# A softmax maximum turned on VectorE instead of TensorE, and value sums added on the way to DRAM

## The chip, the cores and the metric

The kernel runs on one core of one Trainium2 chip. The metric is the device time of one execution in microseconds (us). The engines are named as in the profile: PE (TensorE, the matrix engine), DVE (VectorE), ACT (ScalarE), POOL (GpSimd) and SP (the sync engine, which here only issues DMAs). "PEld" is PE's loading of weights, which overlaps its matmuls. DMAs are issued by SP, ACT and POOL, each with a queue of its own; a queue's engine issues in program order, so a DMA that must wait holds up those behind it.

## The reference

One block of a diffusion transformer on x of shape (2, 2048, 576), in fp32, with 16 heads of D = 36:

```python
ada = silu(c) @ W_ada + b_ada
shift_msa, scale_msa, gate_msa, shift_mlp, scale_mlp, gate_mlp = split(ada, 6)
h = layernorm(x) * (1 + scale_msa) + shift_msa
q, k, v = split(h @ W_qkv + b_qkv, 3)              # 16 heads of 36
attn = softmax((q * 36**-0.5) @ k.T)               # 2048 keys
x = x + gate_msa * ((attn @ v) @ W_proj + b_proj)
h = layernorm(x) * (1 + scale_mlp) + shift_mlp
x = x + gate_mlp * (gelu_tanh(h @ W_fc1 + b_fc1) @ W_fc2 + b_fc2)
```

The softmax takes off a maximum before the exponential. The kernel works with scores that lie keys by queries, so that maximum (one for each query) runs across partitions.

## The kernel before

**Front.** Up to about 270 us the kernel makes the ada vectors, the queries, keys and values of the first batch element (generators `queries_keys_values`, `stages`) and gated copies of two weights. Beside the stages runs a generator `later()`: each `next(rest, None)` in the stages' loop lets it go on to its next `yield`. It loads two sixths of W_ada (`wa`, L202 to L204), yields, clears a PSUM tile (`cleared(2)`), yields, and then makes the rows of ada from it (`rows_of`, matmul L425, tile `pa`), which the gates need.

**Main loop.** The rest is one loop over steps G. A unit is one head of one block of 512 queries (QB); there are NU = 128 units, and each takes NG = 4 steps g = 0 to 3. A step treats 512 of the 2048 keys, two tiles of 128 from each half of them. In one step PE makes the scores of unit su, two units ahead (L648, tile `s`, PSUM), then some matmuls of other work, then the weighted sum of values of the present unit u (L719, tile `av`). The other work is taken from a list: projections of the second batch element (`pq`, `pv`), and for each block whose heads are done the output projection (`po`), the MLP (`pf` L1172 and `py` L1220) and its gathering. `fill()` takes work while a credit lasts, in every even step and in odd ones if the credit is high.

The other engines, for one unit and group of keys:

- ACT copies the scores to SBUF (L661, tile `e`, 128x1024, twice).
- DVE takes the running maximum of them into `acc` (`maxima`, L666). After the fourth group it takes the larger of its two halves (128x512), which leaves for each query 128 candidates, one in each partition.
- In the next step (g = 0 for the present unit, variable `chain`) PE turns these 128x512 by four transposes into PSUM (`turn`, L684, tile `mt`, which takes a buffer of the scores' pool). DVE reduces them to 128x4 (`across`, L694, tile `mx`). SP writes this to DRAM (L695, `m_d`) and reads it back as a broadcast over all partitions (L698, tile `m`, 128x512, two buffers).
- DVE subtracts `m` from the scores (`less`, L703), two steps ahead of PE's use; ACT takes the exponential in place (L707), one step ahead; PE uses it.

`av` has two banks, one for each row half of the array, and in each bank the two halves of the keys lie in partitions 0 to 36 and 64 to 100. So four partial sums are to be added. After the last group `take` has ACT copy one bank to SBUF (L731, tile `up`, one buffer) and DVE add the other (L732). `store`, put off to the end of the next step, has SP write the lower part to DRAM (L738 `o_d`, L739 `sum_d`) and POOL add the upper part to it by accumulating DMAs (L740, L741). Row 0 of each part is the sum of exponentials (`sum_d`), rows 1 to 36 the values.

When the last head of a block is stored, `gather` reads `sum_d` and `o_d` back (L1047 to L1057), loads x with the bias (L820, L824), takes the reciprocal (L1062), writes it (L1063, `rec_d`) and reads it back as broadcasts (L1075, tile `r`) for a multiplication on DVE (L1084). These DMAs are POOL's.

SP's order in a unit: keys and queries of a unit ahead (`kT`, `qT`, L169 and L170), `mx` out (L695), `m` in (L698), then the present store (L738, L739).

Of the kernel before, what the change touches and what calls it, by code (L numbers as in the profile page):

```python
# [10 lines left out]
F32 = mybir.dt.float32  # L11
AF = mybir.ActivationFunctionType
ALU = mybir.AluOpType
AX = mybir.AxisListType
# [3 lines left out]
P = 128  # L18
# [4 lines left out]
def dit_block_kernel(  # L23
# [16 lines left out]
    nc = tc.nc  # L40
# [9 lines left out]
    QB = 512  # L50
    NQB = L // QB
    TB = QB // P
    HA = D + 1
# [3 lines left out]
    NG = HALF // (2 * P)  # L57

    def seq(ins):

        return tc.keep_in_program_order(ins)
# [21 lines left out]
    m_d = [scratch.tile([P, TB], F32, name=f"m_d{u}") for u in range(NB * H)]  # L83

    ident = const.tile([P, P], F32, name="ident")
# [88 lines left out]
    with ExitStack() as front:  # L174
# [200 lines left out]
        def load_in(n):  # L375
# [22 lines left out]
            out=of_b,  # L398
            in_=ident.rearrange("p (k q) -> p q k", k=NC)[:, 0:B, :],
            op=ALU.add,  # L400
            axis=AX.X,
# [3 lines left out]
        def cleared(part):  # L405
            pa = wide(f"pa_{part}")
            seq(nc.vector.memset(pa[:, :, :C2], 0.0))
            return pa
# [108 lines left out]
        def later():  # L517
# [4 lines left out]
            for b in range(B):  # L522
                for i, src in enumerate((b_fc2, b_proj)):
                    at = ds(64 * b + 32 * i, 1)
                    seq(nc.gpsimd.dma_start(out=lines[at, :], in_=src.unsqueeze(0)))
            yield
            yield
            yield
            pas[2] = cleared(2)
            yield  # L530
            g1 = []
# [8 lines left out]
            for b in range(B):  # L540
                seq(nc.vector.tensor_scalar_mul(half[b], g2[b], 0.5))
                for i, (to, g) in enumerate(((gb_d, g2), (gp_d, g1))):
                    at = ds(64 * b + 32 * i, 1)
# [55 lines left out]
    with ExitStack() as main_part:  # L599
# [12 lines left out]
        class Unit:  # L612
# [50 lines left out]
            def maxima(self, g):  # L663

                one, two = (self.es[g][:, j].rearrange("p i n -> p (i n)") for j in range(2))
                top = lambda out, x, y: seq(nc.vector.tensor_max(out, x, y))  # L666
                if g == 0:
                    self.acc = np_.tile([P, 2 * QB], F32, tag="acc", name=f"acc_{self.u}", bufs=1)
                    top(self.acc, one, two)
                    return  # L670
                a = self.acc
                top(a, a, one)
                top(a, a, two)
                if g == NG - 1:
                    self.am = a[:, :QB]
                    top(self.am, a[:, :QB], a[:, QB:])

            def turn(self):

                room = ps_s.tile([P, 2, 512], F32, tag="s", name=f"mt_{self.u}")  # L680
                self.pt = room[:, 0, :].rearrange("p (i n) -> p i n", i=TB)
                for i in range(TB):
                    seq(
                        nc.tensor.transpose(  # L684
                            self.pt[:, i, :],
                            self.am.rearrange("p (n i) -> p i n", i=TB)[:, i, :],
                            ident,
                        )
                    )

            def across(self):

                mx = np_.tile([P, TB], F32, tag="mx", name=f"mx_{self.u}")
                seq(nc.vector.tensor_reduce(out=mx, in_=self.pt, op=ALU.max, axis=AX.X))  # L694
                seq(nc.sync.dma_start(out=m_d[self.u], in_=mx))  # L695
                self.m = np_.tile([P, QB], F32, tag="m", name=f"m_{self.u}")
                flat = m_d[self.u].rearrange("p i -> (p i)")
                seq(nc.sync.dma_start(out=self.m, in_=flat.partition_broadcast(P)))  # L698

            def less(self, g):  # L700
# [26 lines left out]

            def take(self):

                self.up = np_.tile([P, QB], F32, tag="up", name=f"up_{self.u}", bufs=1)  # L730
                seq(nc.scalar.copy(self.up, self.av[:, 0, :]))  # L731
                seq(nc.vector.tensor_add(self.up, self.up, self.av[:, 1, :]))  # L732

            def store(self):

                o, sums = o_d[self.blk][ts(self.h, D), :], sum_d[self.blk][ds(self.h, 1), :]
                lo, hi = self.up[:HA, :], self.up[64 : 64 + HA, :]
                seq(nc.sync.dma_start(out=o, in_=lo[1:HA, :]))  # L738
                seq(nc.sync.dma_start(out=sums, in_=lo[0:1, :]))  # L739
                seq(nc.gpsimd.dma_start(out=o, in_=hi[1:HA, :], accum_op=ALU.add))  # L740
                seq(nc.gpsimd.dma_start(out=sums, in_=hi[0:1, :], accum_op=ALU.add))  # L741

        NT3 = 3
        state = {"wpr": None, "turn": 0, "slot": None, "norm": None}
# [567 lines left out]
        def subtract(G):  # L1312
            if 0 <= G < NU * NG:
                units[G // NG].less(G % NG)
# [17 lines left out]
        for G in range(-AHEAD, NU * NG + 1):  # L1332
# [5 lines left out]
                units[su + 1].load_keys()  # L1338
            if g == 1 and -1 <= u and u + 1 < NU:
                units[u + 1].load_values()  # L1340
            cu, cg = divmod(G - 1 + AHEAD, NG)
            chain = cg == NG - 1 and 0 <= cu < NU
            count(RATE)
            forced = g % 2 == 0 or G < 0 or credit > RATE
            tiles = units[su].scores(sg) if su < NU else None
# [8 lines left out]
            if 0 <= G + 1 < NU * NG:  # L1354
                lu, lg = divmod(G + 1, NG)
                units[lu].exps(lg)
            if chain:
                subtract(G + 2)
                units[cu].turn()
            for last in lasts:  # L1360
                last()
            lasts.clear()
            if 0 <= G < NU * NG:
                units[u].weigh(g)
            if chain:
                units[cu].across()
                if tiles:
                    units[su].maxima(sg)
            elif g == NG - 2:
                if tiles:  # L1370
                    units[su].maxima(sg)
                subtract(G + 2)
            else:
                subtract(G + 2)
                if tiles:
                    units[su].maxima(sg)
            flush()
# [75 lines left out]
```

## Time and profile before

| what | value |
|---|---|
| runs (three) | 3707.89, 3703.1, 3703.63 us, median 3703.63 |
| profiled execution | 3707.24 us, span 3705.5 us |
| granted TensorE clock | 0.999 |
| instructions | 59239 |
| DMA | 382.13 MB, mean 103 GB/s |
| ACT: copy of scores L661 | 1024 of 1025 ns |
| DVE: subtraction L703 | 512 of 2276 ns |
| DVE: maximum L666, 128x1024 | 896 of about 1222 ns |

The profile is of one execution; its own time is 3.6 us above the median of the runs. A row of a group gives the line, the engine, the operation, output and input tiles, their shapes and the count, then the busy time in us and the mean ns of one, then the engine's idle time just before these instructions and what ended it. In a timeline a row starts with its start and its length in us, counted from the start of the span; "x24" joins 24 instructions.

### The profile page before, as it was taken

The page shows a single profiled execution, that of the slowest core. Times are in us where ns is not written, and L with a number is a line of the kernel's source. Part 1 is how long each engine was busy: PE and PEld are TensorE (multiplying, and loading weights), DVE is VectorE, ACT ScalarE, POOL GpSimd, SP SyncE. Part 2 cuts the span into 40 slices and gives each one's busy share as a digit, 9 for nine tenths or more (in the row PEclk, how much of TensorE's full clock was granted, in tenths as well). Part 3 has the DMA queues.
Part 4 walks back from the last instruction along what each step waited for, and adds up shares of the span by engine and source line. Part 5 has one row for each costly group of instructions (what it writes and reads, how often), then busy time and mean ns, then how long its engine had stood idle before and what let it go on. Part 6 is the DMA issues. An engine that isn't in the chain of part 4 may idle for free.

```text
span 3705.5 us, 59239 instructions
## 1 busy us (share of the span) xinstructions
PE 3682.3 (99%) x23926; PEld 1722.0 (46%) x23926; DVE 2948.0 (80%) x3000; ACT 2327.3 (63%) x2166; POOL 706.2 (19%) x1044
## 2 busy tenths in 40 slices
PE   8999999999999999999999999999999999999999
PEld 4554344444444534454444444453444444444565
DVE  4627889889888888888889888988889888988422
ACT  0006767668776677667667777767667767676321
POOL 0101121222122111311131212211130213111411
PEclk9999999999999999999999999999999999999999
DMA  7733333544244343524353424424352435342522
GB/s 245 267 110 105 100 99 96 119 116 111 67 109 112 76 90 80 126 66 99 79 133 70 113 65 114 108 60 105 76 126 67 99 82 120 80 97 61 136 71 70
DMA packets 426946, 382.13 MB, mean 103 GB/s; under 512 B 315591, under 2 KB 316633, under 8 KB 426673
## 3 DMA queue, kind: packets, MB, share of 16 engines
q0 software_dynamic: 77248, 205.28, 20.5%
q1 hardware_dynamic: 82928, 129.54, 12.5%
q10 hardware_dynamic: 266496, 43.53, 7.2%
q8 instruction: 189, 3.10, 0.4%
q14 instruction: 85, 0.69, 0.1%
HBM read 306.98 MB, written 71.21 MB: 102 GB/s over the span
## 4 chain that ended last, share of the span: by engine, by line
PE 94%; DMA 3%; DVE 1%; ACT 1%; issue 1%; POOL 0%; SPq 0%; DVEq 0%; ACTq 0%; POOLq 0%
PE av L719 23%; PE s L648 22%; PE py L1220 15%; PE pf L1172 14%; PE po L799 4%; PE pq_q L975 3%; PE pq L278 3%; PE pf L104 2%; PE pv L328 2%; PE pv_q L799 2%; PE mt L684 2%; DMA x_b<-gp_d 1%; PE po L104 1%; DMA wa<-in_L_cond_W_ada_dram 1%; DVE acc L666 0%
## 5 line engine op out<-in xcount | busy, mean ns | idle before, releaser
L661 ACT COPY e<-s 128x1024 f32<-128x1024 f32 x1024 | 990.2, 1025 | 813.3 <-PE s L648 802.7
L703 DVE TENSOR_TENSOR e<-e,m 128x2048 f32<-128x2048 f32 x512 | 1162.8, 2276 | 9.8 <-DMA m<-m_d 9.8
L666 DVE TENSOR_TENSOR acc<-acc,e 128x1024 f32<-128x1024 f32 x768 | 939.5, 1223 | 171.9 <-ACT e L661 127.7
L707 ACT ACTIVATE e<-e 128x2048 f32<-128x2048 f32 x512 | 991.2, 1936 | 0.9 <-DVE e L703 0.8
L719 PE MATMUL av<-e,v 64*64 64x512 f32 x8192 | 981.3, 594 | 0.1
L648 PE MATMUL s<-qT,kT 36*64 36x512 f32 x8192 | 973.4, 589 | 2.1 <-DVE mx L694 1.1
L1220 PE MATMUL py<-w,gT 128*128 128x288 f32 x2304 | 580.2, 410 | 0.0
L648 PEld LDWEIGHTS s<-qT,kT 36*64 36x64 f32 x8192 | 313.1, 133 | 571.3 <-issue 522.8
L719 PEld LDWEIGHTS av<-e,v 64*64 64x64 f32 x8192 | 296.0, 133 | 510.0 <-issue 460.3
L1172 PE MATMUL pf<-h_b,w_b 128*128 128x512 f32 x1152 | 530.7, 605 | 0.0
L1220 PEld LDWEIGHTS py<-w,gT 128*128 128x128 f32 x2304 | 432.4, 190 | 175.4 <-issue 37.2
L740 POOL DMA_DIRECT2D o_d<-up x128 | 109.3, 854 | 1969.8 <-DMA o_d<-up 1439.2
L1172 PEld LDWEIGHTS pf<-h_b,w_b 128*128 128x128 f32 x1152 | 208.2, 190 | 318.0 <-issue 303.7
L694 DVE TENSOR_REDUCE mx<-mt 128x4 f32<-128x512 f32 x128 | 88.2, 689 | 169.9 <-PE mt L684 169.9
L1183 ACT ACTIVATE gT<-pf,bias 128x512 f32<-128x512 f32 x144 | 99.1, 688 | 193.0 <-PE pf L104 132.7
L1192 DVE SCALAR_TENSOR_TENSOR th<-th,gT 128x1024 f32<-128x1024 f32 x72 | 88.1, 1223 | 90.0 <-ACT th L1190 89.8
L666 DVE TENSOR_TENSOR acc<-e 128x1024 f32<-128x1024 f32 x128 | 155.6, 1216 | 4.4 <-ACT e L661 4.4
L1232 DVE TENSOR_TENSOR x_b<-py,x_b 128x288 f32<-128x288 f32 x192 | 81.5, 452 | 84.2 <-PE py L1220 84.2
L741 POOL DMA_DIRECT2D sum_d<-up x128 | 144.0, 1125 | 1.0 <-issue 1.0
L799 PE MATMUL po<-wpr_p,oT 128*128 128x288 f32 x512 | 132.6, 413 | 0.0
L278 PE MATMUL pq<-hT,w_in 128*128 128x512 f32 (+1 forms) x320 | 129.2, 555 | 0.0
L766 POOL DMA_DIRECT2D w_b<-in_L_cond_W_fc_dram x72 | 73.8, 1025 | 266.9 <-PE pf L1172 242.9
(156 smaller groups left out, 2453.2 us busy)
## 6 DMA issues: line engine op xcount, KB each, us to landing
w<-w_d POOLq DMA_DIRECT2D x72, 576.0 KB, 6.1
v<-v_d ACTq DMA_DIRECT2D x128, 296.0 KB
kT<-qk_d SPq DMA_DIRECT2D x256, 144.0 KB
w_b<-in_L_cond_W_fc_dram POOLq DMA_DIRECT2D x72, 512.0 KB, 4.6
m<-m_d SPq DMA_DIRECT2D x128, 256.0 KB
qT<-qk_d SPq DMA_DIRECT2D x256, 72.0 KB
w_d<-wg POOLq DMA_DIRECT2D x12, 864.0 KB, 8.4
qk_d<-ev SPq DMA_DIRECT2D x36, 256.0 KB
```

The costliest lines, as they stand in the source:

```text
L104: nc.tensor.matmul(outs[r][ts(c, 64), :], lhsT=lefts[r][:, ts(c, 64)], rhs=rights[r], start=starts[r], stop=not starts[r],)
L278: nc.tensor.matmul(pq[:, r, :n], lhsT=w_in[:, kc, cols], rhs=hT[:, kc, at], start=(kc == 0 and not (two and r)), stop=(kc == KC - 2 and tw ...
L648: nc.tensor.matmul(s[ts(c, 64), i, :], lhsT=self.kT[at, ds((2 * g + j) * P + 64 * c, 64)], rhs=self.qT[at, :], start=True, stop=True,)
L661: seq(nc.scalar.copy(self.es[g][:, j], s))
L666: top = lambda out, x, y: seq(nc.vector.tensor_max(out, x, y))
L703: seq(nc.vector.tensor_sub(e, e, m))
L707: seq(nc.scalar.activation(e, e, AF.Exp))
L719: nc.tensor.matmul(self.av[ts(i, 64), r, :], lhsT=self.v[ts(r, 64), ds((c + i * (HALF // P)) * HA, 64)], rhs=e[ts(r, 64), j, i, :], start= ...
L741: seq(nc.gpsimd.dma_start(out=sums, in_=hi[0:1, :], accum_op=ALU.add))
L799: nc.tensor.matmul(outs[n][:, :C2], lhsT=src[:, kc, ts(i, P)], rhs=w_[:, kc, ts(n, C2)], start=(kc == 0), stop=False,)
L1172: nc.tensor.matmul(pfs[j], lhsT=wc[:, kc, ts(j, P)], rhs=h2[:, kc, :], start=(kc == 0 and j == 0), stop=(kc == KC - 2 and j == 1),)
L1220: nc.tensor.matmul(py[n][:, :C2], lhsT=gTs[f - f % 2][:, f % 2, ts(i, P)], rhs=w2s[f - f % 2][:, f % 2, ts(n, C2)], start=(j == 0), stop=( ...
```

## The change

The maximum is turned on DVE. After the last group `maxima` calls `across` at once: DVE transposes the 128x512 in squares of 32x32, reduces each to 128x16, copies the four partition groups of 32 side by side, reduces again to 32x16 and lets SP write this to DRAM. Nothing of it is left on PE. The broadcast read is a step of its own, `load_maxima`, in step g = 1, after the subtraction there, and `m` has one buffer. `take` is one copy of both banks on ACT, and `store` writes one part by SP and adds three by POOL. In the front `later()` has two yields more before `cleared(2)`.

```diff
@@ def later():
             yield
+            yield
+            yield
             pas[2] = cleared(2)
@@ class Unit, maxima
                 if g == NG - 1:
-                    self.am = a[:, :QB]
-                    top(self.am, a[:, :QB], a[:, QB:])
-
-            def turn(self):
-                room = ps_s.tile([P, 2, 512], F32, tag="s", name=f"mt_{self.u}")
-                self.pt = room[:, 0, :].rearrange("p (i n) -> p i n", i=TB)
-                for i in range(TB):
-                    seq(
-                        nc.tensor.transpose(
-                            self.pt[:, i, :],
-                            self.am.rearrange("p (n i) -> p i n", i=TB)[:, i, :],
-                            ident,
-                        )
-                    )
-
-            def across(self):
-                mx = np_.tile([P, TB], F32, tag="mx", name=f"mx_{self.u}")
-                seq(nc.vector.tensor_reduce(out=mx, in_=self.pt, op=ALU.max, axis=AX.X))
-                seq(nc.sync.dma_start(out=m_d[self.u], in_=mx))
-                self.m = np_.tile([P, QB], F32, tag="m", name=f"m_{self.u}")
+                    top(a[:, :QB], a[:, :QB], a[:, QB:])
+                    self.across(a)
+
+            def across(self, a):
+                v = a[:, QB:].rearrange("p (i n) -> p i n", n=32)
+                seq(nc.vector.transpose(v, a[:, :QB].rearrange("p (n i) -> p i n", n=32)))
+                n16 = QB // 32
+                mq = a[:, :n16]
+                seq(nc.vector.tensor_reduce(out=mq, in_=v, op=ALU.max, axis=AX.X))
+                m4 = a[:32, n16 : 5 * n16].rearrange("p (r i) -> p r i", r=4)
+                for r in range(4):
+                    seq(nc.vector.tensor_copy(m4[:, r], mq[ts(r, 32), :]))
+                mx = np_.tile([32, n16], F32, tag="mx", name=f"mx_{self.u}")
+                by_query = m4.rearrange("p r i -> p i r")
+                seq(nc.vector.tensor_reduce(out=mx, in_=by_query, op=ALU.max, axis=AX.X))
                 flat = m_d[self.u].rearrange("p i -> (p i)")
+                seq(nc.sync.dma_start(out=flat.rearrange("(n i) -> n i", n=32), in_=mx))
+
+            def load_maxima(self):
+                flat = m_d[self.u].rearrange("p i -> (p i)")
+                self.m = np_.tile([P, QB], F32, tag="m", name=f"m_{self.u}", bufs=1)
                 seq(nc.sync.dma_start(out=self.m, in_=flat.partition_broadcast(P)))
@@ take, store
-                self.up = np_.tile([P, QB], F32, tag="up", name=f"up_{self.u}", bufs=1)
-                seq(nc.scalar.copy(self.up, self.av[:, 0, :]))
-                seq(nc.vector.tensor_add(self.up, self.up, self.av[:, 1, :]))
+                self.up = np_.tile([P, 2, QB], F32, tag="up", name=f"up_{self.u}", bufs=1)
+                seq(nc.scalar.copy(self.up, self.av))
...
-                lo, hi = self.up[:HA, :], self.up[64 : 64 + HA, :]
-                seq(nc.sync.dma_start(out=o, in_=lo[1:HA, :]))
-                seq(nc.sync.dma_start(out=sums, in_=lo[0:1, :]))
-                seq(nc.gpsimd.dma_start(out=o, in_=hi[1:HA, :], accum_op=ALU.add))
-                seq(nc.gpsimd.dma_start(out=sums, in_=hi[0:1, :], accum_op=ALU.add))
+                for r in range(2):
+                    for at in (0, 64):
+                        part = self.up[at : at + HA, r, :]
+                        for to, rows_ in ((o, part[1:HA, :]), (sums, part[0:1, :])):
+                            if r == 0 and at == 0:
+                                seq(nc.sync.dma_start(out=to, in_=rows_))
+                            else:
+                                seq(nc.gpsimd.dma_start(out=to, in_=rows_, accum_op=ALU.add))
@@ main loop
-            cu, cg = divmod(G - 1 + AHEAD, NG)
-            chain = cg == NG - 1 and 0 <= cu < NU
...
-            if chain:
-                subtract(G + 2)
-                units[cu].turn()
             for last in lasts:
                 last()
             lasts.clear()
             if 0 <= G < NU * NG:
                 units[u].weigh(g)
-            if chain:
-                units[cu].across()
-                if tiles:
-                    units[su].maxima(sg)
-            elif g == NG - 2:
+            if g == NG - 2:
                 if tiles:
                     units[su].maxima(sg)
                 subtract(G + 2)
             else:
                 subtract(G + 2)
+                if g == 1 and -1 <= u and u + 1 < NU:
+                    units[u + 1].load_maxima()
                 if tiles:
                     units[su].maxima(sg)
```

## The prediction

> **What bounds the kernel now.** I read the page's busy shares first.
>
> ```profile
> span 3705.5 us, 59239 instructions
> ## 1 busy us (share of the span) xinstructions
> PE 3682.3 (99%) x23926; PEld 1722.0 (46%) x23926; DVE 2948.0 (80%) x3000; ACT 2327.3 (63%) x2166; POOL 706.2 (19%) x1044
> ```
>
> TensorE (PE) has 23 us without work in the whole span, so a microsecond of PE work taken away is a microsecond of time, unless another engine then falls behind. Next come the groups by line and shape, for what the diff touches.
>
> ```profile
> L684 PE MATMUL mt<-ident,acc 128*128 128x128 f32 x512 | 81.6, 282 | 4.9 <-DVE acc L666 3.0 <-ACT e L661 1.9
> ...
> L694 DVE TENSOR_REDUCE mx<-mt 128x4 f32<-128x512 f32 x128 | 88.2, 689 | 169.9 <-PE mt L684 169.9
> ...
> L732 DVE TENSOR_TENSOR up<-up,av 128x512 f32<-128x512 f32 x128 | 87.5, 683 | 17.6 <-ACT up L731 17.5
> ```
>
> The last two numbers of a row are the engine's idle time before it and who ended it: VectorE (DVE) loses 169.9 us waiting for PE's transposes. Busy PE time overlaps at its modelled ends, so I price the transposes by start times in a timeline of PE, one pair of steps without and one with them.
>
> ```profile
> 1522.42 6.09 PE L1220 MATMUL py<-w,gT 128*128 128x288 f32 x24
> 1528.44 1.95 PE L719 MATMUL av<-e,v 64*64 64x512 f32 x16
> ...
> 1535.47 6.09 PE L1220 MATMUL py<-w,gT 128*128 128x288 f32 x24
> 1541.39 0.63 PE L684 MATMUL mt<-ident,acc 128*128 128x128 f32 x4
> 1541.96 1.52 PE L719 MATMUL av<-e,v 64*64 64x512 f32 x12
> ```
>
> From py to av it is 6.02 us without the four transposes and 6.49 with them: 0.47 us of the path per unit. Last, two windows behind places where PE does wait (length; busy time of PE, PE's weight loads, DVE, ACT, POOL; then the granted clock, DMA share, GB/s), and the SP queue around one unit's end.
>
> ```profile
> 2737.00:2741.00 4.00, 3.88 (x22) 1.59 (x26) 4.00 (x5) 0.00 (x0) 1.26 (x3) 0.63 0.39 109
> ```
> ```profile
> 40.80:44.80 4.00, 3.99 (x21) 1.14 (x22) 0.29 (x1) 0.00 (x0) 0.00 (x0) 0.59 1.04 361
> ```
> ```profile
> 1516.21 0.34 SPq L695 DMA_DIRECT2D m_d<-mx  x1
> 1522.06 0.34 SPq L698 DMA_DIRECT2D m<-m_d  x1
> 1522.46 0.90 SPq L738 DMA_DIRECT2D o_d<-up  x1
> ```
>
> The first window follows a wait of 1.93 us for DVE before transposes at 2737.12, the second a wait of 3.11 us for ada weights (wa) before L425 at 40.81; in both the clock is granted at 0.6 for 4 us afterwards. The SP rows show that a unit's store, ready when L732 ended at 1509.68, leaves at 1522.46 only, behind the load of the maximum, which waits for mx to land.
>
> **The change, part by part.**
>
> *Transposes off PE.* 128 units x 0.47 us = 60.2 us of pure path. With them go PE's waits before them, 4.9 us, and a wait of scores for mx, 1.1 us (list of waits: "PE s L648 <- DVE mx L694"). After the 1.93 us wait 4.00 us ran at 0.63, so 1.5 us more were lost there. Sum 67.7 us.
>
> *Two yields in the front.* In the new order the third pair of query-key matmuls (16 + 8, some 8 us) stands ahead of the ada rows that waited; its weights were sent before wa on the same queue. The rows come 8 us later, when wa (landed by 40.8) is there. Gain 3.1 us and, at 0.59 for 4.00 us, 1.6 us: 4.7. If another load is late there, it is 0.
>
> [...]
>
> *DVE's new chain.* Removed per unit: 0.69 (L694) + 0.68 (L732). Added: a 32x32 transpose of 128x512, a reduction of 128x512, four copies of 32x16, a reduction of 32x64. The reduction has its row, 0.69. No transpose is in the trace: the shortest row of that size is a one-source 128x576 at 454 ns, the nearest above that could stand for a slow pass is 128x2048 at 2.28 us; I take 0.69, that of both 128x512 rows with SBUF input and of the reduction. Copies lie between a memset of 128x16 (72 ns) and a copy of 128x22 (173 ns): 0.16 each. The last reduction lies between 128x8 (159 ns) and 128x512 (689 ns): 0.22. Sum 2.24 us (1.6 to 4.4), net +0.87 per unit (+0.2 to +3.0), +111 us on DVE: 3059, still 84% of a span of 3635. Against that DVE no longer waits for mt and up (169.9 + 17.5 us, 1.46 per unit). The tightest common stretch is a unit like 1314.0 to 1336.6: PE full, DVE 21.28 busy and 1.0 waiting for mt. Afterwards DVE needs 22.15 in 22.13: even. Three such units stand in a row and then units of 26 us with DVE at 22 follow. The pair of subtractions at 1325.23 is taken by ScalarE (ACT) 2.7 and 4.6 us after each is done, at 1330.23 and 1334.32, and the first of these is done 4.5 us before PE uses it (1336.62): that covers the 0.02, and nearly also 2.2 us a unit at the upper end. Cost 0; with the transpose at its upper end up to 2 us in each of 8 blocks, 16.
>
> [...]
>
> *One buffer of m.* The load is issued after the last subtraction of the unit before (step 1) instead of at once, and SP waits there; behind it SP has only the next mx, two steps later. First use is the subtraction of step 2. Between them DVE does four maxima: 1520.26 to 1525.46, 5.2 us. A load landed in 3.00 us in the chain (897.44), and 1522.06 to 1525.46 held one without idle time, so it is hidden by about 2 us. The slowest like it, the 288 KB broadcast x_b<-gp_d, takes 8.8: then DVE idles 3.6 us, which its slack of about 4 us a unit takes up. Cost 0 (0 to 10 us in all).
>
> *The take.* ACT copies 128x1024 (1025 ns, as L661) for 128x512 (589): +56 us on ACT, 63 to 66%. It then frees av by itself, some 0.3 us earlier than copy and add did; the next av is 5 us off. Cost 0.
>
> *Stores.* Per unit four more POOL DMAs, 2 x 0.85 + 2 x 1.13 = 4.0 us, so POOL goes from 706 to 1213 us, 33%. Each add to o_d waits for the one before it: issue to landing 2.7 us (2.1 to 6.6). From the take's end: SP's store 2.7, two adds of 0.5 + 2.7, the third's issue 0.5 and behind it the last sum, 0.6 + 2.6: 12.8 us. But the store is no longer behind the load of m and leaves at about 1509.7 instead of 1522.46, so the chain ends near 1522.5, where now it ends at 1526.74 + 0.6 + 2.6 = 1530. The buffer up, single, is wanted by the next take at 1534.99: 12 us of cover. Behind the adds on POOL stand weight loads of the next steps, no later than now. In a block's second unit the adds stand behind r loads that wait for rec_d (1522.73), so the chain ends near 1533 and the cover is 2 us, with the other r loads 3 us later. 8 blocks at 0 to 3 us: I take 3 us in all. The gather of each block starts some 1.5 to 8 us earlier, which takes the r loads out of the wait that led to 2737.
>
> **Sum.** 67.7 + 4.7 - 3 = 69.4 us off. The profiled execution took 3707.24 us around a span of 3705.5; its runs have a median of 3703.63, 3.6 lower. 3707.24 - 69.4 = 3637.8, on the median 3634.2.
>
> **Rivals.** *Part of it comes back* (12%): PE is free earlier than DVE and ACT can feed it. For it: units at 97% DVE (unit span 2509.6 to 2532.3, 21.9 of 22.65). Against it: 188 us of DVE waits fall away. Price: 16 us there with the long transpose, 24 in the blocks' second units and no 4.7 in the front leave 69.4 + 3 - 44.7 = 27.7 us, 3676, so 3660 to 3690. *The stores decide, slower* (9%): the place is the single buffer up, ACT's take waiting for the fourth landing. The chain holds 3.1 us of copy, issues and wake-ups and four landings L in a row. A unit takes 24.6 us (tile m's uses run from 312.2 to 3457.2, over 128), 24.1 without transposes; with 3 us of slack behind the take the chain exceeds it at L = 6.0, and the gain of 0.54 us a unit is eaten at L = 6.15. At the largest landing of the trace, 6.6, it would be 2.4 us x 128 = 307 us, 3940. Against it: the median is 2.7; for it: three times as many adds share the queue. *The diff's PE saving was cover for something else* (2%): PE waits the 0.47 us elsewhere, 3703. *More* (5%): the transposes are worth their busy 81.6 us, 3613 or less.
>
> **How the numbers follow.** The forecast, 3615 to 3660, has 72%. The range 3615 to 3672 adds about half of the partial case and leaves some 20% outside. Faster by over 0.2% (7 us, about what a measurement of this kernel can tell from no change) is 72 + 12 + 5 = 89%, within it 2%, slower 9%.
>
> **What would show it.** Right: no group mt on PE, PE still at 99% of a span near 3633 and its busy time near 3610; DVE near 3060 us with an idle time before L666 that names ACT, the transpose near 0.7 us; the SP store about 1 us after the take; the row at 40.81 without its wait. Wrong: ACT's copy of up waiting for o_d or sum_d for over 100 us in all, DVE's subtraction waiting for m for over 100 us, PE's idle time above 50 us, or a transpose of over 4 us.

## The result and the profile after: 59 us slower, not 69 us faster

The changed kernel takes 3765.15 us (median of 5 runs, 3762.57 to 3772.67) beside 3705.88 us for the kernel before (5 runs, 3703.1 to 3711.14). The ratio is 1.0161, 95% interval 1.0146 to 1.0176. The prediction was 3634 us, with a range of 3615 to 3672. The profiled execution took 3762.57 us, and its mean granted TensorE clock was 0.987 instead of 0.999.

The page's head, to be held against the first fence of the prediction:

```profile
span 3760.8 us, 59490 instructions
PE 3664.8 (97%) x23414; PEld 1655.4 (44%) x23414; DVE 3124.1 (83%) x3640; ACT 2380.2 (63%) x2166; POOL 1117.9 (30%) x1556
```

PE had 23 us without work before and has 96 now. Its busy time fell by 17.5 us only, though 81.6 us of transposes are gone: what is left runs partly at the slow clock (0.987 in the mean; 0.50 in a window below). The list of PE's waits says whom it waits for (us in total, times, longest):

```profile
PE av L722 <- ACT up L734: 24.8, 7, 10.4
PE py L1225 <- DVE x_b L1237: 20.7, 5, 7.0
PE s L650 <- ACT e L663: 15.3, 12, 3.4
PE po L804 <- DVE x_b L1114: 12.1, 4, 4.9
PE py L1225 <- DVE x_b L1114: 5.0, 3, 3.1
```

No wait is frequent; a few dozen carry everything. Two kinds stand out: `av`, not released because ACT's copy `up` could not start, and PSUM banks of the second part (`po`, `py`), not released because DVE's additions into `x_b` were late. The third row is a kind of its own: in six of its twelve cases, 10.9 of the 15.3 us, ACT had itself stood 1.3 to 6.8 us just before, in a wait that the profile ends with the landing of `m_d<-mx`. No run takes that wait apart.

Cutting both traces at the first av matmul of each unit puts a size on it. 98 of 127 units are shorter, 89 of them by just the 0.47 us of the prediction (22.65 to 22.19, for example). Counted from that shorter length, 22 units lose 113.7 us, and all others together 2.8. The unit from 728 to 752 us of the trace before, the second of a block, went from 23.67 to 32.62 us; six more at the starts of later blocks lose 3.6 to 10.1 us each; these seven hold 48 us of the loss.

**One such place.** Timelines of POOL, ACT, PE and DVE, and then windows (length; busy time of PE, PEld, DVE, ACT, POOL; granted clock, DMA share, GB/s):

```profile
736.10 2.07 POOL L1080 DMA_DIRECT2D r<-rec_d  x4 [8.97 <-PE s L650]
...
739.95 0.95 POOL L746 DMA_DIRECT2D o_d<-up  x1
740.50 1.25 POOL L746 DMA_DIRECT2D sum_d<-up  x1
745.02 0.81 POOL L746 DMA_DIRECT2D o_d<-up  x1 [3.27 <-DMA o_d<-up]
...
747.97 0.81 POOL L746 DMA_DIRECT2D o_d<-up  x1 [1.33 <-DMA o_d<-up]
748.49 1.09 POOL L746 DMA_DIRECT2D sum_d<-up  x1
...
749.59 3.15 POOL L1080 DMA_DIRECT2D r<-rec_d  x5
```
```profile
752.18 1.01 ACT L734 COPY up<-av 128x1024 f32<-128x1024 f32 x1 [12.72 <-DMA sum_d<-up]
```
```profile
753.25 3.69 PE L722 MATMUL av<-e,v 64*64 64x512 f32 x16 [10.41 <-ACT up L734]
```
```profile
756.40 0.69 DVE L1089 TENSOR_TENSOR oT<-oT,r 128x512 f32<-128x512 f32 x1 [7.62 <-DMA r<-rec_d]
```
```profile
742.00:752.50 10.50, 0.83 (x2) 0.00 (x1) 6.47 (x11) 0.32 (x1) 6.15 (x11) 0.77 0.52 139
752.50:757.00 4.50, 3.75 (x20) 1.29 (x24) 0.60 (x1) 4.50 (x5) 4.03 (x9) 0.50 0.82 201
```

POOL waits 9 us at the first `r` load (the profile names PE here; for seven like it, 56.5 us in all, it names the landing of `rec_d`). That wait is not new: before the change eight of them took 57.3 us. New is what follows: three rounds of additions instead of one, each held until the one before has landed (3.27 and 1.33 us of waiting in POOL's rows). The next unit's copy waits 12.72 us for the last of them, PE 10.41 us for the copy. The next five `r` loads leave only behind these rounds, and DVE waits 7.62 us for `r`. Afterwards 16 av matmuls take 3.69 us instead of 1.90, at a granted clock of 0.50.

**The other kind**, DVE's and PE's timelines at another unit:

```profile
1224.56 0.69 DVE L668 TENSOR_TENSOR acc<-acc 128x512 f32<-128x512 f32 x1
1225.28 1.04 DVE L685 STREAM_TRANSPOSE acc<-acc 128x512 f32<-128x512 f32 x1
1226.36 0.69 DVE L688 TENSOR_REDUCE acc<-acc 128x16 f32<-128x512 f32 x1
1227.08 0.69 DVE L691 COPY acc<-acc 32x16 f32<-32x16 f32 x4
1227.81 0.25 DVE L694 TENSOR_REDUCE mx<-acc 32x16 f32<-32x64 f32 x1
1227.99 2.27 DVE L706 TENSOR_TENSOR e<-e,m 128x2048 f32<-128x2048 f32 x1
1230.19 1.20 DVE L668 TENSOR_TENSOR acc<-e 128x1024 f32<-128x1024 f32 x1
1231.32 0.80 DVE L1114 TENSOR_TENSOR x_b<-po,x_b 128x288 f32<-128x288 f32 x2
```
```profile
1231.81 5.84 PE L804 MATMUL po<-wpr_p,oT 128*128 128x288 f32 x16 [1.25 <-DVE x_b L1114]
...
1243.05 4.15 PE L804 MATMUL po<-wpr_p,oT 128*128 128x288 f32 x16 [1.32 <-DVE x_b L1114]
```

PE had ended that `po` at 1223.68; DVE, without a gap, has the addition for it behind the 2.78 us of the turning (from 1225.28 to 1228.06), a subtraction and a maximum. The wait of 1.25 us costs 2.9: the same 16 matmuls take 5.84 us instead of 4.15.

### The profile page after: what moved, and what is told of

It reads as the page before. It is cut to its first block, busy times and chain, and to the rows that moved or that the text cites. A ratio compares the mean times of both kernels' runs of the same rounds, so it can differ in the third digit from the quotient of the medians.

```text
span 3760.8 us, 59490 instructions
## 1 busy us (share of the span) xinstructions
PE 3664.8 (97%) x23414; PEld 1655.4 (44%) x23414; DVE 3124.1 (83%) x3640; ACT 2380.2 (63%) x2166; POOL 1117.9 (30%) x1556
## 3 DMA queue, kind: packets, MB, share of 16 engines
q0 software_dynamic: 101824, 224.73, 25.2%
## 4 chain that ended last, share of the span: by engine, by line
PE 67%; DVE 14%; DMA 7%; issue 6%; ACT 3%; POOL 3%; SPq 0%; ACTq 0%; DVEq 0%; POOLq 0%
PE av L722 15%; PE s L650 15%; PE py L1225 12%; PE pf L1177 10%; DVE acc L668 6%; DVE e L706 3%; PE pq L278 3%; PE pq_q L980 3%; PE pv_q L804 2%; PE pv L328 2%; DMA o_d<-up 2%; PE pf L104 1%; ACT e L663 1%; DMA rec_d<-sums 1%; PE po L804 1%
## 5 line engine op out<-in xcount | busy, mean ns | idle before, releaser
L668 DVE TENSOR_TENSOR acc<-acc,e 128x1024 f32<-128x1024 f32 x768 | 938.6, 1222 | 165.9 <-ACT e L663 118.8
L650 PE MATMUL s<-qT,kT 36*64 36x512 f32 x8192 | 981.4, 593 | 16.3 <-ACT e L663 15.3
L746 POOL DMA_DIRECT2D o_d<-up x384 | 316.1, 823 | 1816.3 <-DMA o_d<-up 1099.5
L1225 PE MATMUL py<-w,gT 128*128 128x288 f32 x2304 | 591.7, 416 | 25.8 <-DVE x_b L1237 20.7
L746 POOL DMA_DIRECT2D sum_d<-up x384 | 404.9, 1054 | 29.5 <-DMA sum_d<-up 22.6
L734 ACT COPY up<-av 128x1024 f32<-128x1024 f32 x128 | 129.9, 1015 | 93.0 <-DMA sum_d<-up 67.8
L685 DVE STREAM_TRANSPOSE acc<-acc 128x512 f32<-128x512 f32 x128 | 135.7, 1060 | 4.4
```

Source lines behind the costliest of these rows:

```text
L650: nc.tensor.matmul(s[ts(c, 64), i, :], lhsT=self.kT[at, ds((2 * g + j) * P + 64 * c, 64)], rhs=self.qT[at, :], start=True, stop=True,)
L685: seq(nc.vector.transpose(v, a[:, :QB].rearrange("p (n i) -> p i n", n=32)))
L746: seq(nc.gpsimd.dma_start(out=to, in_=rows_, accum_op=ALU.add))
L1225: nc.tensor.matmul(py[n][:, :C2], lhsT=gTs[f - f % 2][:, f % 2, ts(i, P)], rhs=w2s[f - f % 2][:, f % 2, ts(n, C2)], start=(j == 0), stop=( ...
```

## The experiments

All ratios are to the kernel before, run beside on the same chip. "Turning" means DVE's chain of transpose, reduction, copies and reduction.

**The parts alone.**

*Old stores.* The changed kernel, `take` and `store` as before:

```diff
-                self.up = np_.tile([P, 2, QB], ...)
-                seq(nc.scalar.copy(self.up, self.av))
+                self.up = np_.tile([P, QB], ...)
+                seq(nc.scalar.copy(self.up, self.av[:, 0, :]))
+                seq(nc.vector.tensor_add(self.up, self.up, self.av[:, 1, :]))
...
```

> The changed kernel with the take and the stores of before (ACT copies one bank, DVE adds the other, one add on the way to DRAM); DVE's turning, the late load of m and the two yields stay. Theory D (DVE's longer chain delays the additions that free PE's PSUM banks): DVE gets 0.68 us a unit more, so it stays slow, 3740 to 3790 us, PE's waits for x_b at 40 us or more; only the waits of av for up vanish. Theory S (the stores' chain in the gather units is the cost): below 3660 us.

Measured 3756.78 us, 1.0138 (1.0124 to 1.0152). The time lies in theory D's range, but D's sign was the wrong one: PE's waits for x_b fell from 40 us to under 3, and those of `av` for `up`, which were to vanish, took their place (PE's waits):

```profile
PE av L722 <- DVE up L735: 87.7, 60, 5.5
```

`av` is released by DVE's addition again, and that stands behind the turning. Without the new stores the change still costs 53 us (3756.8 less 3704.0).

*New stores alone.* The kernel before with the new `take` and `store` and the later load of `m`; the transposes stay on PE.

> The kernel before with the new take and stores; PE's transposes stay. There is room for only one buffer of m, so the load of m is in step 1 here too, as in the run e3_split_load. Theory S: slower than e3_split_load by 40 us or more, with ACT's copy of up waiting for sum_d about 70 us and PE's av for up about 25. Theory D: within 25 us of it, PE waits less for DVE since its addition of 0.68 us a unit is gone.

Measured 3767.27 us, 1.0166 (1.0152 to 1.0179), PE's transposes included. PE's waits:

```profile
PE mt L684 <- ACT e L661: 25.2, 14, 10.7
PE s L648 <- DVE mx L694: 7.2, 6, 2.0
PE mt L684 <- DVE acc L666: 7.0, 5, 2.1
```

ACT's copy of up waited 54.0 us for sum_d (19 times), and what ACT did next, the scores, came late at PE: 21.7 of the 25.2 us in the first row stand just behind such a wait for `sum_d` or `o_d`.

*The later load of m, one buffer,* and *the two yields*, each alone on the kernel before:

> The kernel before, with only the load of m moved to step 1 and one buffer of m; transposes on PE, take and stores of before. Theory M (the single buffer makes DVE wait for m, or SP's new order hurts): 3725 us or more. Otherwise, which theories D and S both hold: 3690 to 3712 us.

> The kernel before with the two yields more in the front and nothing else. Prediction's step: 4.7 us faster (3701), PE's wait of 3.11 us at 40.81 gone and no slow clock behind it. Otherwise 3706 or more.

Measured 3701.29 us, 0.9991 (0.9981 to 1.0), and 3706.33 us, 1.0001 (0.9992 to 1.0009). The buffer costs nothing. The yields take the wait of 3.1 us at 37 us away: none of the 16 profiles with them has it, and two of the three without them do (the kernel before and the new stores alone, not the load of `m`). But the time shows no gain. The first unit begins at 318.3 to 325.2 us in the profiles with the yields (325.2 with the yields alone) and at 321.4 to 324.2 in those without.

So the stores alone cost 66 us over the run with the load of `m` (3767.3 less 3701.3), the turning with old stores 53 over the kernel before, both together 59. They do not add up.

**Place or length of the turning.**

*Turning last.* `across` called behind the x_b additions (`dones`), stores as changed:

```diff
-                    self.across(a)
...
             for done in dones:
                 done()
+            if tiles and sg == NG - 1:
+                units[su].across(units[su].acc)
```

> The changed kernel with one thing moved: a unit's turning of the maxima on VectorE (transpose, reduce, four copies, reduce) is issued behind the additions (x_b) that release PE's banks of the second part, not ahead of them. Nothing is left out. Theory P (place): PE's waits for x_b, 42 us in the profile of the changed kernel (py 26, po 12, others 4), come from the 2.7 us chain standing in front of those additions on an engine that works in order; moved behind, they fall under 10 us, the granted clock rises from 0.987 towards 0.993, and the time falls from 3765 to 3700-3725; the waits of av for ACT's copy of up (25 us, behind stores) stay. Theory L (length): VectorE is too full in runs of units, whatever stands first; the waits move to the subtractions or the next unit's x_b, and the time stays at 3750-3765.

*Without the transpose.*

> The changed kernel without VectorE's 32x32 transpose: the reduce behind it reads the untransposed maxima, so the maxima subtracted are not the queries' own; everything else runs as in the changed kernel. It takes 128 x 1.06 = 136 us off VectorE, and shortens the chain in front of the x_b additions from 2.7 to about 1.6 us. Theory L (length): the time falls by half or more of the loss, to 3715-3735, with VectorE's share down from 83% to 80%. Theory P (place): what stays in front still makes PE wait, PE's waits for x_b fall from 42 to 20-30 us, the time is 3735-3750. Theory S (only the stores decide): 3755-3765.

*Old stores, turning last* (behind the addition that releases av):

> The changed kernel with the stores and the taking of av as before (ACT copies one half, VectorE adds the other, two accumulating stores) and the turning of the maxima issued behind the x_b additions and behind that taking of av. Nothing is left out. Beside the run with the old stores alone (3756.8 us, 88 us of PE waiting for VectorE's addition into up): theory P (place): the wait of av for up falls from 88 to under 30 us and x_b's stays under 5; the time falls to 3640-3700, under the kernel before (3704). Theory L (length): VectorE's 85% leaves no place that costs nothing; the waits turn up at the subtractions and the time is 3730-3757.

Measured: 3748.67 us, 1.0124 (1.0109 to 1.0139); 3715.45 us, 1.0025 (1.0015 to 1.0036); 3687.61 us, 0.9954 (0.994 to 0.9969). With the changed stores the place gave 16 us, between the two theories: PE's waits for x_b fell from 40 us to 28, not under 10. With the old stores it gave 69 us, as theory P had it, and brought the kernel under the kernel before; PE's waits for `up` fell from 87.7 to this:

```profile
PE av L721 <- DVE up L734: 27.1, 31, 2.6
```

DVE did the same work in both (3204.0 and 3185.7 us busy, 86% in the second), so the 69 us are place. Without the transpose, 136 us less on DVE gave 50 us, in theory L's range; PE's waits for x_b fell to 16 us, further than theory P had it. But the turning still stood in front there, so this run shortens what PE waits behind and does not separate length from place.

*ACT takes both halves, GpSimd adds* and then *VectorE adds*, both in SBUF with two accumulating stores and the turning last:

> As the run with the old stores and the turning last, but ACT copies both halves of av (as in the changed kernel) and GpSimd adds them in SBUF, with VectorE out of it: 128 additions of 128x512 (0.68 us each on VectorE, 87 us) leave VectorE, av is released by ACT, and only two accumulating stores a unit are left. Nothing is left out. Theory P (place) and theory S (six accumulating stores cost the waits of up and of the block's second unit) together: PE's waits for up and x_b under 15 us, the time 3630-3670. If GpSimd's addition is slow (over 4 us) or disturbs VectorE, the single buffer of up holds ACT and the time is 3690-3740. Theory L: 3690-3720, since VectorE is 87 us less full than with the old taking.

> As the run with GpSimd's additions, but VectorE adds the two halves that ACT has copied, in SBUF, behind the turning of the maxima; two accumulating stores a unit, as in the kernel before. Nothing is left out. VectorE does as much as in the run with the old stores and the turning last (3687.6 us, where PE waited 27 us, 31 times, for VectorE's addition to release av); here av is released by ACT. Theory P (a step costs where PE waits for it, not by its length): these 27 us go, with the half clock behind them, and the time is 3650-3670. Theory L (VectorE's fullness, 86%): the waits turn up elsewhere and the time stays at 3680-3695. Theory C (ACT's longer copy, 1.02 for 0.65 us, costs by itself): 3680-3700, with PE waiting for ACT's exponentials or its copies of scores.

```diff
                 seq(nc.scalar.copy(self.up, self.av))
+                seq(nc.gpsimd.tensor_add(self.up[:, 0], self.up[:, 0], self.up[:, 1]))
```

Measured 3729.12 us, 1.0067 (1.0052 to 1.0082), and 3693.37 us, 0.9958 (0.9941 to 0.9975). Both miss the times hoped for from place (3630 to 3670 and 3650 to 3670). GpSimd's 128 additions took 1.64 us each, and with them in the kernel DVE's maxima took longer, so that of its 87 us only 13 were won (3185.3 us busy, 3198.5 with DVE adding). DVE's groups with GpSimd adding; without it the rows are 692 and 1222 ns:

```profile
L668 DVE TENSOR_TENSOR acc<-acc 128x512 f32<-128x512 f32 x128 | 111.6, 872 | 4.4
L668 DVE TENSOR_TENSOR acc<-acc,e 128x1024 f32<-128x1024 f32 x768 | 969.6, 1262 | 151.4 <-ACT e L663 104.6 <-DVE acc L668 1.4 <-ACT e L709 0.5
```

The 32x16 copies took 181 ns, 168 in the run with the old stores and the turning last; the subtractions took 2279 and 2270, the transposes 1059 and 1052. Why the maxima grew so much more than these, no run shows. DVE's busy time does not explain why this run is 36 us slower than the one with DVE adding, which is busier. PE waited 29.1 us for ACT's copies of scores there (6.6 with DVE adding), 25.3 of them just after a wait of ACT, nearly all of these ended by the landing of `m_d<-mx` (46.3 us in all, 14.1 with DVE adding). With DVE adding, PE's waits for `up` were 1.0 us, but those for x_b 26.3: the time stood where the run with the old stores and the turning last was, as theory L had it. Theory C's range holds it too, and PE's waits for ACT's copies of scores rose from 2.9 to 6.6 us; the run does not separate the two.

*Three copies* (the first is not needed: its data already lies in place), with ACT taking both halves, and with the old stores:

```diff
-                m4 = a[:32, n16 : 5 * n16].rearrange("p (r i) -> p r i", r=4)
-                for r in range(4):
+                m4 = a[:32, : 4 * n16].rearrange("p (r i) -> p r i", r=4)
+                for r in range(1, 4):
```

> As the run in which ACT takes both halves and VectorE adds them, but with three copies of 32x16 in a unit's chain instead of four: the reduced maxima of the first 32 partitions already stand where the last reduce reads. Nothing is left out. It takes 128 x 0.167 = 21 us off VectorE. Theory P: nothing waits for the chain where it now stands, so the time is within 5 us of the other run. Theory L: VectorE is the bound in the full stretches, and the time falls by 10 to 21 us.

> As the run with the old stores and the turning last (3687.6 us), with three copies of 32x16 in a unit's chain instead of four, 21 us less on VectorE. Nothing is left out. The turning stands behind the addition that releases av, so by theory P (place) its length reaches PE only through the next slots: 0 to 6 us gained, 3682-3688. Theory L (length): 10 to 18 us gained, 3669-3678, as three copies gained 13 us where ACT takes both halves.

*Additions first* (x_b before the slot's maxima, on top of the first of these):

> As the run with three copies (3680.5 us), but in each slot (except the one before a unit's last) VectorE is given the x_b additions of the second part ahead of the slot's maxima, not behind them. Same work, other order; nothing is left out. In the run before, PE waited 20 us for x_b (9 times, up to 5.1) where the maxima of 1.22 us each had piled up in front of the additions. Theory P (place): these waits fall under 8 us and the units 37, 54, 70, 86, 100 and 116 shorten by 2 to 4 us each; the time is 3655-3672. Theory L (length): the units are as long as VectorE's work in them and the time stays within 6 us of 3680. If the additions now wait for PE with VectorE idle, maxima and subtractions come later and the time is over 3690.

Measured 3680.49 us, 0.9924 (0.9908 to 0.9941); 3679.92 us, 0.992 (0.9905 to 0.9936); 3686.47 us, 0.9945 (0.9927 to 0.9963). 21 us off DVE gave 13 us, in theory L's range, and 8 us, between both theories. The other order gave nothing: PE's waits for x_b were 26 us instead of 19, the two longest in the same units. So even with the turning last, DVE's work is not free: 0.4 to 0.6 us for each us taken off (8 and 13 of 21). This price is rough, since runs of one of these kernels lie 3 to 9 us apart.

**The stores.**

*r loads on SyncE*, the changed stores, turning last:

> As the run with the turning last and the changed kernel's six accumulating stores (3748.7 us), with one thing changed: a block's loads of the reciprocals (r) are issued by SyncE instead of GpSimd, so that GpSimd's accumulating stores of the block's first unit no longer stand behind them. In the run before, GpSimd waited 9 to 10 us at the first r load of a block, the adds came out at 744 us where the unit ended at 730, and the next unit took 33 us instead of 23. Nothing is left out. Theory S1 (the adds are late because they are queued behind the r loads): PE's waits of av for up fall from 28 us to under 8, the long units 17, 33, 64, 80, 97, 113 shorten by 3 to 10 us each, and the time falls to 3695-3715. Theory S2 (six adds landing one behind the other are too long by themselves): under 10 us is gained, 3738-3750. If SyncE's own waits now hold the maxima's load, VectorE's subtraction waits for m and the time is above 3750.

Measured 3772.82 us, 1.0173 (1.0157 to 1.0188). PE's waits for `up` fell from 28.4 to 13.0 us and ACT's longest from 13.1 to 5.5, but SP now waited at the r loads and the maxima came late (DVE's waits, 16.9 us in the run compared with):

```profile
DVE e L705 <- DMA m<-m_d: 72.7, 9, 11.2
```

The run shows a new wait, and does not settle the question.

*One round*: `for r in range(1)` in `store`, all else as with the turning last.

> As the run with the turning last and the changed kernel's stores (3748.7 us), but a unit's second row half of sums (r = 1, four of the six accumulating stores) is not written: what is left out is half of the sums of exponentials and values. ACT still copies both halves; the two accumulating stores left stand at the same place of GpSimd's queue, behind a block's r loads. Theory S1 (queued too late): up is still held, PE's waits of av for up stay over 15 us, the time is 3725-3748. Theory S2 (three rounds one behind the other): these waits go to under 4 us, VectorE's wait for the sums (30 us) falls under 10, the long units 17, 33, 64, 80, 97 and 113 are as short as in the run with three copies, and the time is 3670-3700.

Measured 3657.18 us, 0.9863 (0.9847 to 0.9879), the shortest of all, with half of the sums not written: 91 us from four fewer accumulating stores a unit. The two that are left stand at the same place behind the r loads, so that place by itself is not what costs. What PE waits for now, and DVE:

```profile
PE av L721 <- ACT up L733: 1.0, 1, 1.0
PE po L803 <- DVE x_b L1113: 3.0, 2, 1.8
```
```profile
DVE oT L1088 <- DMA r<-rec_d: 24.0, 9, 7.8
```

*Two buffers*: four plain and four accumulating stores, so nothing waits for more than one landing, and the block's loads add the second buffers.

```diff
+                for at in (0, 64):
+                    for r, (od, sd) in enumerate(((o_d, sum_d), (o2_d, sum2_d))):
...
+            for od, sd, how in ((o_d, sum_d, {}), (o2_d, sum2_d, {"accum_op": ALU.add})):
+                seq(nc.gpsimd.dma_start(out=sums, in_=flat_rows(sd[k]), **how))
```

> As the run with the turning last and the changed kernel's taking (ACT copies both halves, VectorE adds nothing), with three copies in the chain, and the stores in two chains: the parts of r = 0 go to o_d and sum_d, those of r = 1 to buffers of their own in DRAM, each with one plain and one accumulating store (four plain on SyncE, four accumulating on GpSimd in a unit), so that no part waits for more than one landing before it; a block's loads then read o_d and sum_d and accumulate the second buffers on top. Nothing is left out. Theory S2 (rounds in series were the cost): the units stay as short as in the run with one round (3657.2 us), the three copies give 0 to 13 us more, and the second loads of a block cost 0 to 10 us in eight blocks' sums: 3645-3670, under the kernel before and under every complete version so far (3680). Theory S1 (number of accumulating stores and their place in GpSimd's queue): four instead of two bring back a part of the 91 us that one round took off; over 3690.

Measured 3733.82 us, 1.0071 (1.0059 to 1.0083): theory S2 as put there falls too, and the time is in S1's range. PE's waits for `up` are 13.1 us, but DVE waits as long as with three rounds, at a block's start:

```profile
DVE oT L1092 <- DMA r<-rec_d: 55.2, 13, 16.4
DVE sums L1070 <- DMA sums<-sum_d: 28.3, 8, 4.2
```

In the changed kernel, and before the change:

```profile
DVE oT L1089 <- DMA r<-rec_d: 56.4, 16, 14.0
DVE sums L1067 <- DMA sums<-sum_d: 31.0, 8, 4.7
```
```profile
DVE oT L1084 <- DMA r<-rec_d: 31.2, 9, 8.4
DVE sums L1062 <- DMA sums<-sum_d: 5.4, 4, 2.9
```

DVE takes its work in order: standing at the reciprocal or a multiplication by r whose data has not landed, it lets subtractions and x_b additions wait that PE needs. In the changed kernel it stood 7.62 us for r up to 756.40, and the subtraction behind that multiplication began at 757.01.

*The block's steps later*: the reciprocal one slot, the r loads and multiplications two slots more, once with three rounds, once with two buffers.

```diff
             yield
             yield
+            yield
             seq(nc.vector.reciprocal(sums, sums))
             seq(nc.gpsimd.dma_start(out=flat_rows(rec_d[k]), in_=sums))
             yield
+            yield
+            yield
```

> The changed kernel's six accumulating stores and its taking of av, the turning of the maxima last, three copies, and at a block's start the reciprocal of the sums one slot later and the loads and multiplications by r two further slots later (each slot is 5.5 us of PE work). Nothing is left out. In the changed kernel VectorE waits 31 us for sums and 56 us for r in eight blocks, and GpSimd's adds of a block's first unit stand behind the r loads. Theory B (the block's start: VectorE and GpSimd wait in order for data that has not landed): VectorE's waits for sums and r fall under 25 us together, PE's waits of av for up (28 us) under 8, and the time is 3660-3700, against 3730-3745 for the same kernel without the delay (3748.7 with four copies). Theory N (number of stores: GpSimd and the DMA rounds are too long wherever they stand): less than 15 us is gained, 3725-3748.

> The run with two buffers (3733.8 us), with the same delay of the block's steps: reciprocal one slot later, loads and multiplications by r two further. Nothing is left out. Theory B: VectorE's waits for sums and r, 83 us, fall under 25, and the time comes near that of one round, 3650-3690. Theory N: 3720-3740.

Measured 3708.02 us, 1.0009 (0.9997 to 1.0022), and 3691.51 us, 0.9958 (0.9944 to 0.9972): both under theory N's ranges, the first 8 us and the second 1.5 above theory B's range. With every transfer kept, two buffers gained 42 us from the later place; DVE's waits for sums and r fell from 83.5 us to

```profile
DVE oT L1095 <- DMA r<-rec_d: 18.9, 5, 10.8
```

and none for sums. With three rounds the time fell 41 us against the run with the turning last, of which the copy left out may have 8 to 13; DVE's waits for r were 12.8 and for sums 0.5. What three rounds still cost there, 17 us, shows most at the single `up`: PE waited 14.6 us for its copy, beside 3.2 with two buffers. So the stores' loss has at least two seats: the block's start, where engines stood waiting for data that the longer chain of landings brought later, and the buffer `up`, held by three landings in a row. The later steps also took GpSimd's waits at the `r` loads for `rec_d` away (66.2 to 14.7 us with two buffers), so which engine's waiting PE paid for at the block's start is not separated. And beside one round, 3657 us with four copies, two buffers still stand 34 us higher; no run explains these.

The best versions that leave nothing out are the two with three copies, 3680 us, 0.992: the change's turning on DVE, put last and one copy shorter, with two accumulating stores.

## Why the prediction was wrong, step by step

- *Transposes off PE, 0.47 us a unit:* right, 89 units show it to the hundredth.
- *DVE's chain, cost 0:* this step failed. Its size was short: the transpose took 1.06 us (estimate 0.69, bounds 0.45 to 2.28), the copies 0.166 each (0.16), the last reduction 0.249 (0.22); the chain 2.66 instead of 2.24. DVE was busy for 3124 us, not 3059. The rows:

```profile
L685 DVE STREAM_TRANSPOSE acc<-acc 128x512 f32<-128x512 f32 x128 | 135.7, 1060 | 4.4
L691 DVE COPY acc<-acc 32x16 f32<-32x16 f32 x512 | 85.2, 166 | 9.6
L694 DVE TENSOR_REDUCE mx<-acc 32x16 f32<-32x64 f32 x128 | 31.9, 249 | 4.4
```

  But the larger fault is the slack. It was read off subtraction, exponential and PE, 4.5 us. That path did hold: PE waited 1.4 us in all for an exponential. But other work in DVE's queue has no such slack: the additions that give PE its PSUM banks back. They were not looked at, nor what would stand in front of them: moving the chain behind them and behind the addition that releases `av` was worth 69 us with the old stores.
- *The take, cost 0:* ACT's 1.02 us was right, and releasing `av` from ACT was indeed worth something: with the old take and the turning where the change puts it, PE waited 87.7 us.
- *Stores, 3 us:* failed; alone they cost 66. The chain of three landings and the second unit of a block, with 2 us of cover, were named, but the price of 0 to 3 us for each was too low: 9.4 us in the first, 3.6 to 10.1 in six others. Wholly missing was DVE at a block's start: the prediction had the gathering begin earlier, and DVE's waits for sums rose from 5.4 to 31.0 us, for r from 31.2 to 56.4.
- *One buffer of m, cost 0:* right (0.9991).
- *Two yields, 4.7 us:* the wait goes, as forecast, but the gain did not come: 0 measured (0.9992 to 1.0009, where 4.7 us would be 0.9987). What takes it up again in the front stays open.
- *Clock:* the prediction credited the slow clock to the waits that go, but gave no price to that of new waits. PE's idle time rose by 73 us, and the rest of the 116.5 us lost, some 44, agrees with the fall of the mean clock, 0.012 of 3761 = 45. Behind the wait of 1.25 us at 1231.81 the clock was granted at 0.59 for 4.2 us; behind that of 1.32 us at 1243.05 it stayed at 1.00. So the length of a wait does not alone say whether the clock falls behind it. The clock records of this trace show more: 17 stretches at half clock in the span, each 3.41, 6.83 or 10.24 us long, with starts that lie whole multiples of 3.413 us from one another (from the first, 570.20, to the last, 3560.28, it is 876 times that). Counted in such steps the wait of 1.25 us lies within one, 1228.98 to 1232.39, at whose end the clock fell, while that of 1.32 us is divided between two, 0.90 and 0.42. In the step before each of the 17 falls PE stood 1.25 us or more; five other steps with 1.3 to 2.0 us had no fall behind them, so this is not the whole rule.

The span adds up from these: 59.7 us less (0.47 x 127) and a front 5.9 us shorter in this execution, against 116.5 us lost in units and 4.5 us behind the last one: 55 us more, as the spans show (3760.8 less 3705.5).

Of the rivals, "the stores decide, slower" had the right mechanism in part (single `up`, waiting landings) with a wrong place, all units at a landing of 6 us; landings were 2.7 us in the median, and the seven units at block starts hold 48 us of the loss. "Part of it comes back" had DVE's full stretches, at 16 us. Of the signs named for wrong, PE's idle time above 50 us came true (96); ACT's copy waiting for o_d or sum_d was 72 us, the subtraction waiting for m 14, so neither mark of 100 was met although the stores were guilty.

What stays open: the split of the stores' loss between `up`, the block's start and ACT's waits ended by `m_d<-mx`. Two buffers took PE's waits for `up` from 28.4 to 13.1 us with DVE's as before, for 15 us of time, of which the copy left out may have 8 to 13; the later steps then took 42 us, and with DVE's waits those for `up` fell too, to 3.2. That puts most of it on the block's start, without measuring it by itself. Open is also why the parts do not add up (59 together, 53 and 66 alone). That they hit the same units, so that one wait covers another, is argued and not shown.

## What to carry to other kernels

Before giving an in-order engine more work, list everything that other engines wait for in its queue, and take the slack of the tightest, at the fullest stretch, not that of the path the change is about; then place the new work behind it. A wait put on the bounding engine costs more than its length where the clock falls after it: 2.9 us for 1.25 here. A transfer that lands later does its harm where an in-order engine meets the instruction that needs it, so it can be mended by issuing that instruction later, with every transfer kept: 42 us with two buffers here.

## What the runs showed of the hardware

- VectorE's transpose of fp32 128x512 in 32x32 squares takes 1.06 us, half more than a reduction of the same data (0.69).
- A chain of dependent steps costs DVE more than its rows: in the changed kernel's timeline from 1214.77 to 1231.32 us, 30 to 40 ns lie between the end of a step of the turning and the start of the next, where unrelated instructions overlap by 70 to 90 ns; the 32x16 copies took 0.166 us each.
- The accumulating stores, 72 KB of values or 2 KB of sums each, landed 2.7 us after issue in the median, 7.3 us at most; the program's next one to the same rows waited for that landing (POOL stood 1099.5 us for `o_d`, 291 times).
- The clock of TensorE fell to half 17 times in the changed kernel's profile, for 3.41, 6.83 or 10.24 us, and by the trace's clock records the falls lie whole multiples of 3.413 us apart; a wait of 1.25 us inside one such step was followed by a fall, one of 1.32 us divided between two was not.
